# Delta u stored by half units in groups of 32 rows, and spread by two matmuls on different rows of the array

## The chip, the cores and the metric

The program runs on one core of a Trainium2 chip. The metric is the device time of one execution in microseconds, the median of several runs; less is better. The engines are named as in the profile: PE is TensorE (its matmuls; PEld are its weight loads), DVE is VectorE, ACT is ScalarE, POOL is GpSimd, SP is SyncE, which here only issues transfers. SPq and ACTq are the issuing of transfers on SP and ACT.

## The reference, cut to what matters

The program computes four layers on x of shape (4, 96, 64, 64). Layer 0 is a selective scan in four directions, layer 1 a deformable convolution, layers 2 and 3 work on the image as tokens. The change is in layer 0. Its inner part, for each image b, direction k, channel d (192 of them) and state n (16 of them), along l = 0 to 4095:

```python
delta = softplus(dts + delta_bias)
dA = exp(delta[..., None] * A)                       # A: channel x state
h = dA * h + (delta * u)[..., None] * B[:, :, None, :]
y = einsum('bkdn,bkn->bkd', h, C)
```

The product delta * u, a vector over channels, is needed for each of the 16 states of a channel. That repetition is what the text calls spreading.

## The kernel before

**Units.** The scan is cut into 1536 units: 4 images, 4 directions, 4 steps of T = 1024 positions, 3 groups g of 64 channels, and 8 units per group. A unit has 8 channels times 16 states on the 128 partitions, and 1024 positions. Partition p stands for state p // 8 and channel p % 8 of the unit. The 8 units of a group are a block; they are numbered s = i + 4q, with i from 0 to 3 and q from 0 to 1, and are taken in the order i, then q.

**Where delta u comes from.** In `steps` (line 750 on) the softplus and the product with u are made in chunks of CH = 512 positions. The product is written as a sum of three bf16 parts (lines 798 to 808) into the tile `du` of shape [128 channels, 3, 512], or of two halves of 64 channels for two directions. Line 812 stores it in the scratch tensor `du_d[b]`, whose shape is [4 directions, 3 parts, 192 channels, 4096], one or two transfers for each chunk step. The step size itself, delta, is stored in `de_d` (line 794).

**What a unit does.**

- `fetch` (line 911, on ACT's queue) loads the decay tile `da`: 8 rows of `de_d`, each of them to 16 partitions, 512 KB in all. It is done five units ahead.
- `fetch_block` (line 926, on SP's queue) loads delta u for the next block: two tiles of 96 rows (3 parts x 32 channels) by 1024 positions in bf16, one for q = 0 and one for q = 1, 192 KB each. It is issued at the third unit of a block.
- `fetch_step` (line 918, SP) loads B and C for a step, once in 24 units.
- `decay` (line 932, ACT) takes the exponential of `da` with the scale `al`, a column of A for each unit.
- `inflow` (line 938, PE) spreads delta u: two matmuls of 96 rows by 128 columns, one for each half of 512 positions, into the two PSUM banks of a tile `db`. The stationary operand `rep` is a matrix of zeros and ones that picks the 8 channels of the unit from the 32 of the tile, and adds the three parts. The same rows of the array serve both halves. There are two such tiles, four of the eight banks.
- `enter` (line 952, DVE) multiplies `db` by B in place, and `recur` (line 960, DVE) runs the recurrence along the positions.
- `weigh` (line 969, POOL) multiplies by C.
- `total` (line 988, PE) adds the 16 states of a channel for two units at once: eight matmuls with 32 columns, into four column groups, with the matrix `fold`, which also puts each channel at its place among 32. `settle` and `store` (lines 999 and 1006) bring the sums to `y_d`.

**What sets the order.** All instructions are written out in program order, engine by engine. Beside the scan two streams of other work (layer 0's own first and last parts, and layers 1 to 3 of the images that are ready) are cut into steps. A planner, the class `Clock`, keeps a planned end for each engine from costs in the source, and lets a step of a stream in between two units if the engines have room. The spreading of a unit costs PE 0.8 us in this plan (line 935), and a unit has a pace of 4.5 us. So the costs change the order of the instructions, nothing else. After the last unit the streams go on alone; that part is called the tail.

**Completion of transfers.** The transfers of SP and ACT count their completions on eight semaphores in turn (read from the built program). A transfer waits until the one before it on its semaphore has landed.

Of the kernel before, what the change touches and what calls it, by code (L numbers as in the profile page):

```python
# [20 lines left out]
L = H * W  # L21
DI, NS, R, KG = 192, 16, 6, 4
D2 = DI - 128
T = 1024
# [20 lines left out]
def prepare(x, **w):  # L45
# [51 lines left out]
    dtp[64 : 64 + R + 1, 2:] = dtw[2:].transpose(2, 0, 1)  # L97
    a["dtw"] = dtp

    al = w["L0_conv_A_logs"].reshape(KG, DI // D8, D8, NS)  # L100
    a["al"] = c(al.transpose(3, 2, 0, 1).reshape(128, KG * DI // D8))

    ds = w["L0_conv_Ds"].reshape(KG, NG, 64).transpose(2, 1, 0)
    a["ds"] = c(np.concatenate([ds, ds]))
# [22 lines left out]
    for n in (2, 3):  # L127
# [14 lines left out]
    a["cen_c"] = wide(cen[128:], 256)  # L142

    p = np.arange(128)
    rep = (p[:, None, None] % 32 == 8 * np.arange(4)[None, :, None] + p[None, None] % 8).astype(f)
    a["rep"] = c(rep)
    a["fold"] = c(
        (p[:, None, None] % 8 + 8 * np.arange(4)[None, :, None] == np.arange(32)[None, None]).astype(f)
    )
    yy, xx = np.divmod(np.arange(L).reshape(32, 128).T, W)  # L150
    ki, kj = np.divmod(np.arange(9), 3)
# [368 lines left out]
class Unit:  # L520


    def __init__(self, b, k, step, g, i, q):
        self.b, self.k, self.step, self.g, self.i = b, k, step, g, i
        self.s = i + 4 * q
        self.back = k >= 2
        self.j = NT - 1 - step if self.back else step
        self.n = 8 * g + self.s
        self.key = f"{b}_{k}_{self.j}_{g}_{self.s}"
        self.first_of_block = i == 0 and q == 0  # L530
        self.first_of_step = self.first_of_block and g == 0
        self.ts = slice(self.j * T, (self.j + 1) * T)
        self.bc = self.du = None
# [5 lines left out]
class Layer0:  # L539
# [7 lines left out]
    def __init__(self, ctx, net, x1):  # L547
        self.net, self.x1 = net, x1
        tc, nc, ins = net.tc, net.nc, net.ins
        wp = ctx.enter_context(tc.tile_pool(name="l0w", bufs=1))  # L550
        for name in ("fold", "al", "ds"):
            setattr(self, name, net.load(name, wp))

        nc.scalar.activation(self.al, self.al, AF.Exp)
        nc.vector.tensor_scalar_mul(self.al, self.al, -1.0)

        dsum = wp.tile([128, NG], F32, name="dsum")
        nc.vector.reduce_sum(dsum, self.ds, axis=mybir.AxisListType.X)
        self.skip = wp.tile([128, NG, 128], F32, name="skip")
        for g in range(NG):  # L560
            nc.vector.tensor_scalar_mul(self.skip[:, g, :], net.ident, dsum[:, g : g + 1])

        self.wc_d = net.dram.tile([C, 9, 256], F32, name="wc_d")
        self.rep = wp.tile([128, 4, 128], BF16, name="rep16")
        self.minus = wp.tile([128, 128], BF16, name="minus")
        nc.vector.tensor_scalar_mul(self.minus, net.ident, -1.0)
        with tc.tile_pool(name="l0prep", bufs=1) as tp:
            nc.vector.tensor_copy(self.rep, net.load("rep", tp))
            w_in = net.load("w_in", tp)
            cw = tp.tile([C, 9, 256], F32, name="cwr")  # L570
            nc.sync.dma_start(cw, ins["cw"].partition_broadcast(C))
            nc.vector.tensor_mul(cw, cw, w_in[:, :256].unsqueeze(1).to_broadcast([C, 9, 256]))
            nc.sync.dma_start(self.wc_d, cw)
        dram = net.dram
        self.u_d = [dram.tile([DI, L], F32, name=f"u{b}") for b in range(B)]
        self.z_d = [dram.tile([DI, L], F32, name=f"z{b}") for b in range(B)]
        self.de_d = [dram.tile([KG, DI, L], F32, name=f"de{b}") for b in range(B)]
        self.du_d = [dram.tile([KG, 3, DI, L], BF16, name=f"du{b}") for b in range(B)]
        self.bc_d = [dram.tile([KG, 2 * NS, L], F32, name=f"bcd{b}") for b in range(B)]
        self.y_d = [dram.tile([KG, DI, L], F32, name=f"y{b}") for b in range(B)]  # L580
        self.sp = ctx.enter_context(tc.tile_pool(name="l0s", bufs=2))
        self.banks = ctx.enter_context(ExitStack())
        self.ps = self.banks.enter_context(tc.tile_pool(name="l0q", bufs=1, space=PSUM))


        self.ready, self.summed = set(), set()

        self.scanned = (0.0, 0.0)

        self.settled = 0.0  # L590
# [160 lines left out]
    def steps(self, b, ks, j, us, dtw, sm, xdbl):  # L751
# [56 lines left out]
        nc.scalar.copy(du[:, 2, :], pr)  # L808
        yield cost(pe=0.4, act=0.6)
        for p0, p1, k, c0 in parts:  # L810
            dst = self.du_d[b][k][:, c0 : c0 + p1 - p0, cs]
            nc.sync.dma_start(dst.rearrange("s c t -> c s t"), du[p0:p1])
        self.ready.update((b, k, both, j) for k in ks)
        yield wait(frees="du")

# [66 lines left out]
    def fetch(self, u, before):  # L882


        sp, nc = self.sp, self.net.nc
        b, k, j, g, ts = u.b, u.k, u.j, u.g, u.ts
        c0 = 64 * g
        halves = [slice(j * T + h * CH, j * T + (h + 1) * CH) for h in range(2)]
        if not u.first_of_step:
            u.bc = before.bc  # L890
        elif u.bc is None:
            self.fetch_step(u)
        if u.first_of_step and u.step == 0:
            u.state = sp.tile([128, DI // D8], F32, name=f"st{u.key}", tag="st")
        else:
            u.state = before.state
        if not u.first_of_block:
            u.du, u.sums = before.du, before.sums
        else:
            u.sums = {"add": None}  # L900
            if u.du is None:
                self.fetch_block(u)
        if u.i == 1 and u.s == 1 and (k == 0 or u.back):
            add = u.sums["add"] = sp.tile([128, CH], F32, name=f"ad{u.key}", tag="ad", bufs=1)
            src = self.y_d[b][k - 2] if u.back else self.u_d[b]
            for h in range(2):
                nc.scalar.dma_start(add[64 * h : 64 * h + 64], src[c0 : c0 + 64, halves[h]])
        self.net.clock.add(ACT, 0.6, self.scanned[1])
        u.da = sp.tile([128, T], F32, name=f"da{u.key}", tag="da", bufs=6)
        src = self.de_d[b][k][c0 + D8 * u.s : c0 + D8 * u.s + D8, ts]  # L910
        nc.scalar.dma_start(u.da, src.unsqueeze(0).to_broadcast([NS, D8, T]))

    def fetch_step(self, u):
# [5 lines left out]

    def fetch_block(self, u):  # L920

        u.du = []
        for q in range(2):
            t = self.sp.tile([96, T], BF16, name=f"du{u.key}_{q}", tag=f"du{q}")
            c0 = 64 * u.g + 32 * q
            self.net.nc.sync.dma_start(t, self.du_d[u.b][u.k][:, c0 : c0 + 32, u.ts])
            u.du.append(t)

    def decay(self, u):
        u.decayed = self.net.clock.add(ACT, 1.15, 0.0)  # L930
# [1 line left out]
        self.net.nc.scalar.activation(u.da, u.da, AF.Exp, scale=self.al[:, a : a + 1])  # L932

    def inflow(self, u):
        u.spread = self.net.clock.add(PE, 0.8, self.scanned[1])
        db = self.ps.tile([128, 2, CH], F32, name=f"db{u.key}", tag="db", bufs=2)
        for h in range(2):
            self.net.nc.tensor.matmul(  # L938
                db[:, h, :],
                lhsT=self.rep[:96, u.s % 4, :],  # L940
                rhs=u.du[u.s // 4][:, h * CH : (h + 1) * CH],
                start=True,
                stop=True,
            )
        u.db = db.rearrange("p h t -> p (h t)")
# [843 lines left out]
```

## Time and profile before

| | |
|---|---|
| timed runs | 9014.61 us median of 3 (9012.24 to 9038.34) |
| profiled execution, span from first to last instruction | 8965.3 us (no other time of that execution is listed) |
| granted TensorE clock, mean | 0.807 |
| PE busy | 6639.1 us (74%) |
| DVE busy | 6689.3 us (75%) |
| ACT busy | 5244.1 us (58%) |
| POOL busy | 5561.5 us (62%) |
| spreading matmuls (line 938), 3072 | 1101.2 us busy |
| transfers | 1608.49 MB, 179 GB/s in the mean |

The timed runs stand about 49 us above the profiled span, which covers first to last instruction alone. A share of busy time is an average over the whole span; the scan runs from about 350 us to 7634 us, and the tail after it has other limits. In the lists of groups, a row gives line, engine, operation, output and inputs, shape and count, then busy time and the mean of one in nanoseconds, then the idle time of the engine just before such instructions and what ended it. A wait is given as "who <- whom: total, times, longest".

### The profile page before, as it was taken

To read this page: it belongs to the slowest core of one execution; us is meant where nothing else is said; L and a number is where in the kernel's file an instruction comes from. 1 tells how busy PE (TensorE), PEld (TensorE's weight loads), DVE (VectorE), ACT (ScalarE), POOL (GpSimd) and SP (SyncE) were. 2 spreads that over 40 slices of the span, in tenths; PEclk is the share of its full clock that TensorE was granted. 3 is DMA by queue.
4 is the path that set the end of the run, shared out by engine and by line. 5 is a ranking of instruction groups with operands and counts; after the bars stand their busy time and mean duration, and the time that the engine had idled before them with its cause. 6 is when DMAs were issued, how large, how long until landed. Compare 5 with 4: busy or idle time off the path is not lost.

```text
span 8965.3 us, 97776 instructions
## 1 busy us (share of the span) xinstructions
PE 6639.1 (74%) x31960; PEld 2926.8 (33%) x31960; DVE 6689.3 (75%) x4995; ACT 5244.1 (58%) x10214; POOL 5561.5 (62%) x4307
## 2 busy tenths in 40 slices
PE   6675967687767678777667888776888777766687
PEld 2111311122222233312223554122455322454373
DVE  0498889987889987788898887898887889223414
ACT  4564656555567767755566665545666665267623
POOL 0365657666668888766688887667888876245200
PEclk8776977798778889877778888787898887867798
DMA  1476777767778888877788888667888876434120
GB/s 51 133 205 173 193 191 220 198 183 181 189 202 231 235 224 228 204 199 194 200 230 219 233 218 213 160 177 193 215 229 222 216 188 156 104 108 131 57 62 12
DMA packets 776001, 1608.49 MB, mean 179 GB/s; under 512 B 247810, under 2 KB 339358, under 8 KB 773383
## 3 DMA queue, kind: packets, MB, share of 16 engines
q10 hardware_dynamic: 244224, 843.17, 36.4%
q1 hardware_dynamic: 457542, 532.51, 22.0%
q0 software_dynamic: 73728, 226.57, 9.6%
q8 instruction: 257, 4.21, 0.2%
q14 instruction: 250, 2.04, 0.1%
HBM read 1345.62 MB, written 256.29 MB: 179 GB/s over the span
## 4 chain that ended last, share of the span: by engine, by line
PE 35%; DVE 27%; DMA 15%; ACT 10%; issue 7%; POOL 2%; SPq 2%; ACTq 1%; another core or an unknown queue 0%; DVEq 0%; POOLq 0%
DVE hh L960 13%; DVE db L952 7%; DMA du<-du 5%; PE pc L691 4%; PE py L988 4%; ACT g L1312 4%; PE ps L1331 3%; PE db L938 3%; PE f L1425 3%; DMA da<-de 2%; PE pd L1347 2%; POOL hh L969 1%; DMA bc<-bcd 1%; ACT da L932 1%; PE h L1466 1%
## 5 line engine op out<-in xcount | busy, mean ns | idle before, releaser
L969 POOL TENSOR_TENSOR hh<-hh,bc 128x1024 f32<-128x1024 f32 x1536 | 3658.6, 2384 | 351.9 <-DVE hh L960 244.2
L960 DVE TENSOR_TENSOR_SCAN hh<-da,st,db 128x1024 f32<-128x1024 f32 x1152 | 2701.1, 2345 | 229.9 <-PE py L988 86.1
L952 DVE TENSOR_TENSOR db<-db,bc 128x1024 f32<-128x1024 f32 x1536 | 1863.4, 1213 | 523.2 <-PE db L938 517.9
L932 ACT ACTIVATE da<-da,w_al 128x1024 f32<-128x1024 f32 x1536 | 1741.5, 1146 | 641.0 <-DMA da<-de 287.2
L938 PE MATMUL db<-du,rep 96*128 96x512 bf16 x3072 | 1101.2, 447 | 824.6 <-DVE hh L960 764.5
L1301 POOL DMA_INDIRECT g<-table,idx x1152 | 1151.2, 999 | 546.3 <-issue 195.7
L1312 ACT ACTIVATE g<-g,wt 128x96 f32<-128x96 f32 x4608 | 1282.6, 365 | 146.8 <-DMA du<-du 37.3
L988 PE MATMUL py<-hh,w_fold 128*32 128x512 f32 x6144 | 1055.2, 760 | 24.2 <-POOL hh L969 10.7
L960 DVE TENSOR_TENSOR_SCAN hh<-da,db 128x1024 f32<-128x1024 f32 x384 | 877.3, 2285 | 71.9 <-PE py L988 22.1
L1331 PE MATMUL ps<-w_ident,g 128*96 128x128 f32 x3744 | 682.8, 322 | 300.6 <-ACT g L1312 142.7
L938 PEld LDWEIGHTS <-rep 96*128 96x128 bf16 x3072 | 284.3, 107 | 1772.3 <-issue 1139.0
L780 POOL TENSOR_TENSOR lw<-lw,w 128x512 f32<-128x512 f32 x192 | 244.3, 1273 | 820.9 <-DVE w L778 808.7
L1331 PEld LDWEIGHTS ps<-w_ident,g 128*96 128x96 f32 x3744 | 483.2, 142 | 655.0 <-ACT g L1312 255.2
L967 POOL COPY st<-hh 128x1 f32<-128x1 f32 x1152 | 233.3, 202 | 696.0 <-DVE hh L960 637.4
L691 PE MATMUL pc<-pad,wc 96*128 96x512 f32 x1152 | 548.4, 616 | 53.4 <-DMA wc<-wc_d 46.8
L1339 ACT COPY st<-ps 96x384 f32<-96x384 f32 x384 | 180.2, 472 | 395.5 <-PE ps L1331 301.6
L801 PE MATMUL pr<-ex,w_ident 128*128 128x512 f32 x384 | 281.5, 823 | 173.0 <-DVE ex L791 89.8
L778 DVE SCALAR_TENSOR_TENSOR w<-w,ex 128x512 f32<-128x512 f32 x192 | 159.4, 830 | 285.7 <-ACT w L775 285.6
L1318 DVE TENSOR_TENSOR g<-g 128x576 f32<-128x576 f32 x96 | 72.9, 759 | 390.0 <-ACT g L1312 360.5
L691 PEld LDWEIGHTS pc<-pad,wc 96*128 96x128 f32 x1152 | 217.1, 195 | 336.4 <-issue 305.3
L988 PEld LDWEIGHTS py<-hh,w_fold 128*32 128x32 f32 x6144 | 153.9, 122 | 511.0 <-issue 384.4
L769 PE MATMUL pd<-xd,w_dtw 103*64 103x512 f32 (+1 forms) x512 | 267.1, 800 | 66.5 <-DVE rl L782 27.5
(249 smaller groups left out, 8899.5 us busy)
## 6 DMA issues: line engine op xcount, KB each, us to landing
da<-de ACTq DMA_DIRECT2D x1536, 512.0 KB
du<-du SPq DMA_DIRECT2D x512, 192.0 KB
bc<-bcd SPq DMA_DIRECT2D x128, 512.0 KB
du<-du SPq DMA_DIRECT2D x128, 384.0 KB
y<-yb SPq DMA_DIRECT2D x384, 128.0 KB
de<-rl SPq DMA_DIRECT2D x128, 256.0 KB
m<-in_dft SPq DMA_DIRECT2D x128, 256.0 KB
ad<-y ACTq DMA_DIRECT2D x192, 128.0 KB
```

Of the source, the lines that this page charges most:

```text
L691: nc.tensor.matmul(pp, lhsT=wc[:, q, g * 128 : (g + 1) * 128], rhs=pad[:, r0 + dy : r0 + dy + NR, dx : dx + W], start=(q == 0), stop=(q == 8),
L801: nc.tensor.matmul(pr, lhsT=net.ident, rhs=ex, start=True, stop=False)
L932: self.net.nc.scalar.activation(u.da, u.da, AF.Exp, scale=self.al[:, a : a + 1])
L938: self.net.nc.tensor.matmul(db[:, h, :], lhsT=self.rep[:96, u.s % 4, :], rhs=u.du[u.s // 4][:, h * CH : (h + 1) * CH], start=True, stop=True,)
L952: self.net.nc.vector.tensor_mul(u.db, u.db, u.bc[:, 0, :])
L960: nc.vector.tensor_tensor_scan(u.along(u.hh), u.along(u.da), u.along(u.db), first, ALU.mult, ALU.add)
L969: self.net.nc.gpsimd.tensor_mul(u.hh, u.hh, u.bc[:, 1, :])
L988: nc.tensor.matmul(py[p0 : p0 + 32], lhsT=self.fold[:, u.i, :], rhs=hc[:, h * CH : (h + 1) * CH], start=u.sums["add"] is None and u.i == 0 ...
L1301: nc.gpsimd.indirect_dma_start(out=g[:, k, :], out_offset=None, in_=self.tables[b % 2], in_offset=bass.IndirectOffsetOnAxis(ap=idx[:, n : ...
L1312: nc.scalar.activation(pixel, pixel, AF.Identity, scale=wt[:, n, c : c + 1])
L1331: nc.tensor.matmul(pt[:, k, :], lhsT=g[:, k, c * C : (c + 1) * C], rhs=net.ident, is_transpose=True, start=(c == 0), stop=(c == corners - 1),)
L1425: nc.tensor.matmul(pt[64 * part : 64 * part + 64, c, :], lhsT=d[:, :, c0 + c], rhs=matrix[:, 64 * part : 64 * part + 64], start=True, stop ...
```

## The change

The scratch tensor for delta u is laid out anew: for each direction, chunk of 512 positions and group of 32 channels it holds 96 rows of 512 bf16 numbers, which lie together. Row r = 32 s + c is part s of channel c. A half unit is then loaded as 24 partitions with four rows each: partition p holds the rows 4p to 4p + 3, and the row i of these belongs to the channels c with c % 4 = i. So unit i of a group of 32 channels takes every fourth channel, i, i + 4, and so on, instead of eight neighbours.

- **Store** (line 812 before): one transfer for every 32 channels, in place of one for all the channels of a direction.
- **Load** (line 926): one tile with four pieces of 24 partitions, at partitions 0, 32, 64 and 96, for q = 0 and 1 and the halves h = 0 and 1; four transfers of 96 KB in place of two of 192 KB.
- **Spreading** (line 938): the two matmuls of a unit have 24 rows each, at the partitions 64 q and 64 q + 32. They write the two banks of `db` as before. `rep` is now one matrix for all units.
- **Decay load** (line 911): the 8 rows of `de_d` are every fourth one. The columns of `al` and the matrix `fold` follow the new order of channels.
- **Plan**: the spreading costs PE 0.5 us in place of 0.8.

```diff
@@ -97,8 +97,8 @@
     dtp[64 : 64 + R + 1, 2:] = dtw[2:].transpose(2, 0, 1)
     a["dtw"] = dtp
 
-    al = w["L0_conv_A_logs"].reshape(KG, DI // D8, D8, NS)
-    a["al"] = c(al.transpose(3, 2, 0, 1).reshape(128, KG * DI // D8))
+    al = w["L0_conv_A_logs"].reshape(KG, DI // 32, D8, 4, NS)
+    a["al"] = c(al.transpose(4, 2, 0, 1, 3).reshape(128, KG * DI // D8))
 
     ds = w["L0_conv_Ds"].reshape(KG, NG, 64).transpose(2, 1, 0)
     a["ds"] = c(np.concatenate([ds, ds]))
@@ -142,10 +142,9 @@
     a["cen_c"] = wide(cen[128:], 256)
 
     p = np.arange(128)
-    rep = (p[:, None, None] % 32 == 8 * np.arange(4)[None, :, None] + p[None, None] % 8).astype(f)
-    a["rep"] = c(rep)
+    a["rep"] = c((p[:, None] % 8 == p[None] % 8).astype(f))
     a["fold"] = c(
-        (p[:, None, None] % 8 + 8 * np.arange(4)[None, :, None] == np.arange(32)[None, None]).astype(f)
+        (4 * (p[:, None, None] % 8) + np.arange(4)[None, :, None] == np.arange(32)[None, None]).astype(f)
     )
     yy, xx = np.divmod(np.arange(L).reshape(32, 128).T, W)
     ki, kj = np.divmod(np.arange(9), 3)
@@ -522,6 +521,7 @@
 
     def __init__(self, b, k, step, g, i, q):
         self.b, self.k, self.step, self.g, self.i = b, k, step, g, i
+        self.q = q
         self.s = i + 4 * q
         self.back = k >= 2
         self.j = NT - 1 - step if self.back else step
@@ -561,7 +561,7 @@
             nc.vector.tensor_scalar_mul(self.skip[:, g, :], net.ident, dsum[:, g : g + 1])
 
         self.wc_d = net.dram.tile([C, 9, 256], F32, name="wc_d")
-        self.rep = wp.tile([128, 4, 128], BF16, name="rep16")
+        self.rep = wp.tile([128, 128], BF16, name="rep16")
         self.minus = wp.tile([128, 128], BF16, name="minus")
         nc.vector.tensor_scalar_mul(self.minus, net.ident, -1.0)
         with tc.tile_pool(name="l0prep", bufs=1) as tp:
@@ -575,7 +575,9 @@
         self.u_d = [dram.tile([DI, L], F32, name=f"u{b}") for b in range(B)]
         self.z_d = [dram.tile([DI, L], F32, name=f"z{b}") for b in range(B)]
         self.de_d = [dram.tile([KG, DI, L], F32, name=f"de{b}") for b in range(B)]
-        self.du_d = [dram.tile([KG, 3, DI, L], BF16, name=f"du{b}") for b in range(B)]
+        
+
+        self.du_d = [dram.tile([KG, NCH, DI // 32, 3 * 32, CH], BF16, name=f"du{b}") for b in range(B)]
         self.bc_d = [dram.tile([KG, 2 * NS, L], F32, name=f"bcd{b}") for b in range(B)]
         self.y_d = [dram.tile([KG, DI, L], F32, name=f"y{b}") for b in range(B)]
         self.sp = ctx.enter_context(tc.tile_pool(name="l0s", bufs=2))
@@ -808,8 +810,9 @@
         nc.scalar.copy(du[:, 2, :], pr)
         yield cost(pe=0.4, act=0.6)
         for p0, p1, k, c0 in parts:
-            dst = self.du_d[b][k][:, c0 : c0 + p1 - p0, cs]
-            nc.sync.dma_start(dst.rearrange("s c t -> c s t"), du[p0:p1])
+            for p in range(p0, p1, 32):
+                dst = self.du_d[b][k, j, (c0 + p - p0) // 32].rearrange("(s c) t -> c s t", s=3)
+                nc.sync.dma_start(dst, du[p : p + 32])
         self.ready.update((b, k, both, j) for k in ks)
         yield wait(frees="du")
 
@@ -907,7 +910,7 @@
                 nc.scalar.dma_start(add[64 * h : 64 * h + 64], src[c0 : c0 + 64, halves[h]])
         self.net.clock.add(ACT, 0.6, self.scanned[1])
         u.da = sp.tile([128, T], F32, name=f"da{u.key}", tag="da", bufs=6)
-        src = self.de_d[b][k][c0 + D8 * u.s : c0 + D8 * u.s + D8, ts]
+        src = self.de_d[b][k][c0 + 32 * u.q + u.i : c0 + 32 * u.q + 32 : 4, ts]
         nc.scalar.dma_start(u.da, src.unsqueeze(0).to_broadcast([NS, D8, T]))
 
     def fetch_step(self, u):
@@ -919,12 +922,12 @@
 
     def fetch_block(self, u):
 
-        u.du = []
+        u.du = self.sp.tile([128, 4, CH], BF16, name=f"du{u.key}", tag="du")
         for q in range(2):
-            t = self.sp.tile([96, T], BF16, name=f"du{u.key}_{q}", tag=f"du{q}")
-            c0 = 64 * u.g + 32 * q
-            self.net.nc.sync.dma_start(t, self.du_d[u.b][u.k][:, c0 : c0 + 32, u.ts])
-            u.du.append(t)
+            for h in range(2):
+                p0 = 64 * q + 32 * h
+                src = self.du_d[u.b][u.k, 2 * u.j + h, 2 * u.g + q]
+                self.net.nc.sync.dma_start(u.du[p0 : p0 + 24], src.rearrange("(p i) t -> p i t", i=4))
 
     def decay(self, u):
         u.decayed = self.net.clock.add(ACT, 1.15, 0.0)
@@ -932,13 +935,13 @@
         self.net.nc.scalar.activation(u.da, u.da, AF.Exp, scale=self.al[:, a : a + 1])
 
     def inflow(self, u):
-        u.spread = self.net.clock.add(PE, 0.8, self.scanned[1])
+        u.spread = self.net.clock.add(PE, 0.5, self.scanned[1])
         db = self.ps.tile([128, 2, CH], F32, name=f"db{u.key}", tag="db", bufs=2)
         for h in range(2):
             self.net.nc.tensor.matmul(
                 db[:, h, :],
-                lhsT=self.rep[:96, u.s % 4, :],
-                rhs=u.du[u.s // 4][:, h * CH : (h + 1) * CH],
+                lhsT=self.rep[64 * u.q + 32 * h : 64 * u.q + 32 * h + 24],
+                rhs=u.du[64 * u.q + 32 * h : 64 * u.q + 32 * h + 24, u.i, :],
                 start=True,
                 stop=True,
             )
```

## Prediction

> **What bounds the kernel now.** I read the page first, then the busy time of the stage that the change touches, then the list of waits, then the chain piece by piece.
>
> ```profile
> PE 6639.1 (74%) x31960; PEld 2926.8 (33%) x31960; DVE 6689.3 (75%) x4995; ACT 5244.1 (58%) x10214; POOL 5561.5 (62%) x4307
> ...
> PE 35%; DVE 27%; DMA 15%; ACT 10%; issue 7%; POOL 2%; SPq 2%; ACTq 1%; another core or an unknown queue 0%; DVEq 0%; POOLq 0%
> ...
> L952 DVE TENSOR_TENSOR db<-db,bc 128x1024 f32<-128x1024 f32 x1536 | 1863.4, 1213 | 523.2 <-PE db L938 517.9
> ...
> L938 PE MATMUL db<-du,rep 96*128 96x512 bf16 x3072 | 1101.2, 447 | 824.6 <-DVE hh L960 764.5
> ```
>
> No engine is full over the span; the chain is mostly PE and DVE handing over to each other. Its second line (by line) gives DMA du<-du 5% and PE db L938 3%, the two things that the change touches. The scan runs from 350 to 7634 us:
>
> ```profile
> 350.00:7634.00 7284.00, 5455.65 (x24581) 2175.05 (x24582) 6247.82 (x4239) 4443.47 (x8179) 5228.19 (x3975) 0.81 0.78 203
> ```
>
> The columns after the length are PE, PEld, DVE, ACT, POOL busy, the clock and the DMA share. DVE (third) is busy 86% there, so it sets the pace and only its 7284 - 6248 = 1036 us of idle time can be won in this stage. The waits, each with its total, count and longest:
>
> ```profile
> DVE db L952 <- PE db L938: 517.9, 226, 20.6
> ...
> ACT da L932 <- DMA da<-de: 287.2, 136, 9.8
> ...
> PE db L938 <- DMA du<-du: 40.5, 8, 22.4
> ```
>
> Half of DVE's idle time is the wait for the spread (226 times, 2.3 us each). The pair itself takes 0.61 us, so most of such a wait is PE being late for another reason. One is seen in the chain:
>
> ```profile
> 5169.87 0.55 ACTq L911
> 5170.42 0.05 issue
> 5170.47 0.17 ACT g L1312
> 5170.63 21.44 DMA du<-du
> 5192.07 0.02 issue
> 5192.09 0.02 ACTq L911
> ```
>
> Nothing on ACT reads du here. ACT issues the next decay load (L911), and in the program as built the loads and stores of SP and ACT take eight completion semaphores in turn: each waits for the landing of the one eight before it. A slow du load so stops ACT, and with it whatever PE waits for from ACT. From the issue and completion times in the trace: a du load (192 KB) lands after 12.6 us in the mean (5% above 22.1), a decay load of 512 KB after 7.6 us. ACT's issues stood 425 us in all on such semaphores, 184 us of it (54 times) on a du load.
>
> **What the Trainium skill says.** "DMA: Bandwidth & Descriptors", section "Why a DMA increments its semaphore by 16 and not by 1": a transfer runs on the largest number of engines up to 16 that divides the slowest dimension of both sides. A du load reads 3 x 32 x 1024 into 96 rows, so 3 engines. The trace agrees: 4 increments (3 and the sequencer's rest) at the median against 16 for the others. After the change it is 24 rows on both sides, so 12. "TensorEngine Tiling (Array Packing)", "Key Properties": changing the tiling mode drains TensorE. The trace agrees: from the second spread matmul to a full-array one (L1331, L691) is 215 ns, start to start, to the column-tiled fold (L988) 307 ns; leaving the fold for the spread costs 525 against 429. A switch is 92 to 97 ns. "TensorE: Matmul & The Clock Gate", Part 3: matmuls on different row groups start about 4 ns apart. The trace has no pair on different rows; its column-tiled folds start 6 to 7 ns apart.
>
> **The change part by part.**
>
> *The pair on PE (L938).* Now the second matmul of a pair starts 219 to 226 ns after the first. On different rows and banks I take 7 ns, the fold's figure: 212 x 1536 units = -326 us of PE. The bound on the other side: K=64 matmuls that follow each other on the same rows (L1059) start 533 ns apart where full-array ones need 429, so a weight load that cannot be hidden shows as 104 ns. With a gap of 110 ns it is -167 us. If the two do not overlap at all, 0. Below -326 is excluded, since one of the two still streams.
>
> *Mode switches.* The pair is now a 32-row mode. In the built programs the matmul stream changes mode 2508 times before and 3858 after: +1350 x 92 ns = +124 us of PE. Where PE was waiting anyhow it costs nothing; where the granted clock is half it costs double. PE in sum: -202 us (-43 with the unhidden load, +124 without overlap). PE is 35% of the chain, so **-70 us** (-15 to +43).
>
> *The du loads.* Two of 192 KB on 3 engines become four of 96 KB on 12: per engine 128 KB becomes 32 KB, and the mean landing of 12.6 us, for two that share 3 engines, becomes about 5 us (a quarter of it, and the 2 us that the smallest transfers here take). Three waits shrink. ACT's 184 us on du semaphores: less two thirds, -120. ACT's wait for decay data: a decay load lands in 8.7 us when a du load is in flight (883 of 1536) and 6.2 us when not; the 16-engine load waits for the three busy engines. Most of that difference goes, half of the 287 us: -140. PE's own waits for du, 41 us and 34 more at its weight load: -50. In sum -310 us of engine waits. They lie beside DVE's work except where they reach it; I let the share of the PE chain, 0.35 to 0.4, through: **-120 us** (0, if DVE is held by the next late thing each time, to -250).
>
> *More transfers on eight semaphores.* Loads +384, stores +512 (a step's one or two become four of 32 rows): 2550 on SP become 3446, with 1824 on ACT unchanged. The time until a semaphore comes round, 11.8 us at the median for a decay load before 4750 us, falls by a fifth to 9.8 us. Queued behind are SP's stores of y and loads of bc and, on ACT, the exponentials. The other 241 us of ACT's semaphore waits grow by about a third, +85, of which 0.4 counts: **+35 us** (0 to +150).
>
> *SP's issues.* 896 x 0.63 us (1610 us for 2550 now) = 560 us more, 18% to 24% of the span. Hidden by SP's idle time; without that cover each burst delays the next issue by 1 to 2 us: 0 to +20.
>
> *Decay loads with rows 64 KiB apart instead of 16.* Same 4 KB rows, same 16 engines. The Trainium skill, "DMA: Bandwidth & Descriptors", "Latency and other measured facts", sees copies slow down above a pitch of 512 KiB, not shown here: 0, up to +30.
>
> *Order and planner (0.8 becomes 0.5).* DVE instructions after the last scan fall from 687 to 656: side work comes earlier by little. The sign of a reshuffled order is open: 0, -40 to +40. The multiply now comes before side work on DVE more often (713 such instructions stand between multiply and scan, 640 before): a wait there is the price if the spread is late.
>
> Sum: -70 - 120 + 35 = **-155 us**. The profiled span 8965.3 gives 8810; the page lists no time of that execution beside its span. The median of the timed runs, 9014.61, lies 49.3 us above the span, taken as unchanged: **8860 us**. What is late next is the scan on DVE itself, and PE with the offset and sampling matmuls (L1331, L1425).
>
> **Rivals.**
>
> *Only one half works.* Either the pair overlaps but the switches take it back, or the loads land sooner but DVE waits for something else: about half of the sum, -45 to -85 us, 8930 to 8970. For it: the next waits are close behind (fold's hh buffers 108 us). Against it: two separate mechanisms would have to fail in turn.
>
> *Slower: the semaphores come round too soon.* Bursts of four stores and four loads take half of the eight at once, and ACT waits at its next decay load. It decides if a transfer lands later than the eighth issue after it, 9.8 us: a decay load's 95th percentile is already 11.4 us in the first stage. 192 load bursts and 192 store bursts with 1 us on ACT each are 384 us, times 0.4 is +150; with -70 on PE and the du gain gone, 9014.6 + 80 = 9095, and 9050 if half of the bursts are hit. Against it: the same bytes in smaller pieces land sooner, and the longest holders, the du loads, are the ones cut.
>
> *No overlap on rows.* The matmuls stay 219 ns apart, and the 124 us of switches are added: +43, with -85 from the loads 8970. The profile has no row pair to exclude it.
>
> *Nothing to see.* DVE refills each gap: within 27 us of 9014.6.
>
> **How the numbers follow.** Both halves 0.50 (8860, own range 8780 to 8930); one half or no overlap on rows 0.20 (8930 to 8980); nothing 0.11; slower 0.19 (9050 to 9100). Faster by over 0.3% (27 us, about what a measurement of this kernel can tell from no change) is 0.70, within it 0.11, slower 0.19. The range leaves out about one in ten above and one below: 8760 to 9045.
>
> **What would show it.** Right: the pair's PE row drops from 1101 us busy to about 600 to 750; du loads land in about 5 us; du<-du falls from 5% of the chain to under 2%; ACT's wait for da from 287 to about 150 us; DVE's for db from 518 to 350 to 400; the scan stage ends 130 to 170 us sooner and the tail stays at about 1330 us. Wrong: the matmuls of a pair over 200 ns apart; ACT's semaphore waits above 425 us; or DVE's idle time in the scan unchanged at about 1000 us though both rows improved.

## The result, and the profile after

| | before | after |
|---|---|---|
| timed runs, median | 9013.42 us (4 runs, 8998.19 to 9038.34) | 8902.61 us (4 runs, 8878.90 to 8935.01) |
| profiled span | 8965.3 us | 8907.3 us |
| granted TensorE clock, mean | 0.807 | 0.772 |
| PE busy | 6639.1 us | 6652.8 us |

The medians differ by 111 us, where 154 was forecast. The ratio on record is 0.9894, with a 95% interval of 0.9865 to 0.9923, or 96 us of 9013; it is not the quotient of the two medians, which is 0.9877. All ratios below are of the recorded kind. The two spans differ by 58 us only. In the runs after, an execution takes 1.8 to 1.9 us longer than its span (8909.16 beside 8907.3). So the profiled execution of before took some 8967 us by the same allowance and was a quick one among its runs. The comparisons further on ran on several chips, where the kernel before took between 8940 and 9013 us, so all that is compared across them is compared as a ratio to the runs of before on the same chip. Where an expectation below is in microseconds and reckons from 9013, the ratio is what to hold against it.

From the page of the kernel after, its busy line and four groups (columns as in the rows shown before: busy time, mean ns, idle time before it and what ended that):

```profile
PE 6652.8 (75%) x31960; PEld 2892.8 (32%) x31960; DVE 6650.0 (75%) x4995; ACT 5235.3 (59%) x10214; POOL 5574.2 (63%) x4307
...
L955 DVE TENSOR_TENSOR db<-db,bc 128x1024 f32<-128x1024 f32 x1536 | 1863.3, 1213 | 574.3 <-PE db L941 553.6
L935 ACT ACTIVATE da<-da,w_al 128x1024 f32<-128x1024 f32 x1536 | 1739.3, 1146 | 492.1 <-DMA da<-de 134.6
...
L941 PE MATMUL db<-du,rep 24*128 24x512 bf16 x3072 | 707.8, 459 | 869.5 <-DVE hh L963 803.8
...
L991 PE MATMUL py<-hh,w_fold 128*32 128x512 f32 x6144 | 1119.7, 798 | 20.5 <-POOL hh L972 13.6
```

The spreading fell from 1101 to 708 us busy, 393 us less. But PE as a whole did not fall. Its other work rose from 6639.1 - 1101.2 = 5537.9 to 6652.8 - 707.8 = 5945.0 us, 407 us more, with the same 31960 matmuls. The fold (L991) is one row of it, 798 ns for one after; before it was 760 ns:

```profile
L988 PE MATMUL py<-hh,w_fold 128*32 128x512 f32 x6144 | 1055.2, 760 | 24.2 <-POOL hh L969 10.7
```

ACT's wait for decay data halved, from 287 to 135 us. DVE's wait for the spread was to fall and rose, from 518 to 554 us.

In one stretch of the timeline the two matmuls of a unit begin together and take 0.39 us, with the fold straight after; before, such a pair took 0.61 us:

```profile
5263.69 0.39 PE L941 MATMUL db<-du,rep 24*128 24x512 bf16 x2
...
5264.01 1.06 PE L991 MATMUL py<-hh,w_fold 128*32 128x512 f32 x8
```

Next the scan and the tail. The columns are the window, its length, the busy time and count of PE, PEld, DVE, ACT and POOL, the granted clock, the DMA share and GB/s. This is the kernel after, its windows split at the end of the scan:

```profile
350.00:7652.00 7302.00, 5522.94 (x25493) 2188.44 (x25493) 6235.57 (x4271) 4462.94 (x8229) 5240.55 (x3977) 0.77 0.80 204
7652.00:8907.30 1255.30, 912.64 (x6018) 619.81 (x6018) 375.75 (x655) 616.70 (x1792) 318.79 (x312) 0.77 0.28 78
```

And the kernel before, split at the end of its own scan:

```profile
350.00:7637.00 7287.00, 5458.34 (x24594) 2175.35 (x24594) 6250.69 (x4241) 4443.47 (x8179) 5229.99 (x3975) 0.81 0.78 203
7637.00:8965.30 1328.30, 969.55 (x6916) 668.38 (x6916) 399.61 (x686) 644.73 (x1842) 316.65 (x313) 0.79 0.28 80
```

The scan did not get shorter: it ends 15 us later. DVE is idle 7302 - 6236 = 1066 us in it, where it was 7287 - 6251 = 1036. The tail is 73 us shorter, and some 900 matmuls (25493 against 24594) have moved from the tail into the scan. So three things had to be explained: PE's other work that grew, a scan that gained nothing from better loads, and a gain that shows in the tail.

### The profile page after: what moved, and what is told of

It reads as the page before. It is cut to its first block, busy times and chain, and to the rows that moved or that the text cites. A ratio compares the mean times of both kernels' runs of the same rounds, so it can differ in the third digit from the quotient of the medians.

```text
span 8907.3 us, 98649 instructions
## 1 busy us (share of the span) xinstructions
PE 6652.8 (75%) x31960; PEld 2892.8 (32%) x31960; DVE 6650.0 (75%) x4995; ACT 5235.3 (59%) x10214; POOL 5574.2 (63%) x4307
## 4 chain that ended last, share of the span: by engine, by line
PE 23%; DVE 14%; ACT 9%; DMA 7%; issue 5%; POOL 2%; SPq 1%; ACTq 1%; another core or an unknown queue 0%; DVEq 0%; POOLq 0%
DVE hh L963 7%; ACT g L1315 4%; DVE db L955 3%; PE f L1428 3%; PE ps L1334 3%; PE py L991 2%; DMA da<-de 2%; PE pd L1350 2%; DMA m<-in_dft 1%; ACT da L935 1%; PE db L941 1%; POOL hh L972 1%; PE zp L1494 1%; PE h L1469 1%; PE pc L693 1%
## 5 line engine op out<-in xcount | busy, mean ns | idle before, releaser
L935 ACT ACTIVATE da<-da,w_al 128x1024 f32<-128x1024 f32 x1536 | 1739.3, 1146 | 492.1 <-DMA da<-de 134.6
L941 PE MATMUL db<-du,rep 24*128 24x512 bf16 x3072 | 707.8, 459 | 869.5 <-DVE hh L963 803.8
L991 PE MATMUL py<-hh,w_fold 128*32 128x512 f32 x6144 | 1119.7, 798 | 20.5 <-POOL hh L972 13.6
L941 PEld LDWEIGHTS <-rep 24*128 24x128 bf16 x3072 | 159.5, 93 | 1979.8 <-issue 1222.5
L803 PE MATMUL pr<-ex,w_ident 128*128 128x512 f32 x384 | 320.8, 930 | 178.3 <-DVE ex L793 96.0
L771 PE MATMUL pd<-xd,w_dtw 103*64 103x512 f32 (+1 forms) x512 | 296.7, 879 | 72.6 <-DVE rl L784 31.1
L1350 PE MATMUL pd<-st,wdc 96*128 96x256 f32 x1152 | 327.1, 436 | 9.6 <-DVE rl L784 4.9
```

Source lines behind the costliest of these rows:

```text
L803: nc.tensor.matmul(pr, lhsT=net.ident, rhs=ex, start=True, stop=False)
L941: self.net.nc.tensor.matmul(db[:, h, :], lhsT=self.rep[64 * u.q + 32 * h : 64 * u.q + 32 * h + 24], rhs=u.du[64 * u.q + 32 * h : 64 * u.q ...
L991: nc.tensor.matmul(py[p0 : p0 + 32], lhsT=self.fold[:, u.i, :], rhs=hc[:, h * CH : (h + 1) * CH], start=u.sums["add"] is None and u.i == 0 ...
L1350: nc.tensor.matmul(po, lhsT=wdc[:, k, :], rhs=st[:, k, :], start=(k == 0), stop=(k == 8))
```

## The experiments

The change has four separable parts: loads spread over more DMA engines, more and smaller transfers, the pair on different rows, and the plan value 0.5. My theory was that the loads and the pair both gain. The rivals were that one of the two does nothing, that the transfers take the gain back, or that the plan does more than assumed. The edits are shown cut to the lines that matter for the argument; `...` stands for lines left out.

### The loads alone

The kernel before, with nothing changed but the order of the dimensions of `du_d`, so that one run of 96 rows is read; the store and the matrix `rep` follow that order. Two loads a block and 0.8 in the plan stay.

```diff
-du_d: [KG, 3, DI, L]
+du_d: [KG, DI, 3, L]
...
-dma_start(t, self.du_d[u.b][u.k][:, c0 : c0 + 32, u.ts])
+src = self.du_d[u.b][u.k][c0 : c0 + 32, :, u.ts]
+dma_start(t, src.rearrange("c s t -> (c s) t"))
...
-rep = (p[:, None, None] % 32 == ...)
+rep = (p[:, None, None] // 3 == ...)
...
```

> The kernel before, with delta u stored as [direction, channel, part, position], so that a load of 32 channels has 96 rows in its slowest dimension on both sides (16 engines in place of 3). Two loads of 192 KB and as many stores as before, the spreading on the full array and the plan (0.8) as before. The loads theory (the gain of 111 us comes from du loads that leave three engines): 8900 to 8940 us, du loads landing in 5 to 7 us, ACT's wait for da near 135 us. The pair theory (it comes from the overlap of the two spreading matmuls) and the plan theory (it comes from the cost 0.5): within 27 us of before, 8990 to 9040.

Measured: 8761.58 us, ratio 0.9757 (0.9730 to 0.9784). That is more than the whole change brings, and more than expected. A du load now makes 16 completion increments in place of 4 and lands after 6.5 us in the mean (12.6 before). Decay loads land after 7.0 us (7.6 before), B and C after 10.2 (15.5). ACT stands on completion semaphores for 202 us in place of 425, of which 22 in place of 184 are on du loads. In the list of waits of this kernel (who, for whom, total, times, longest) DVE's wait for the spread is down from 518 us, though PE does the same matmuls:

```profile
DVE db L952 <- PE db L938: 386.4, 193, 17.8
...
ACT da L932 <- DMA da<-de: 208.0, 101, 8.0
```

And its windows, scan and tail:

```profile
350.00:7405.00 7055.00, 5413.64 (x24594) 2165.26 (x24594) 6245.81 (x4240) 4440.99 (x8181) 5234.99 (x3975) 0.81 0.81 210
7405.00:8736.40 1331.40, 973.48 (x6918) 672.40 (x6916) 400.06 (x687) 644.47 (x1842) 317.25 (x313) 0.79 0.28 79
```

The scan ends 232 us earlier and the tail is untouched. So the late loads had been in the path of the scan all along.

### The change without the better loads

The kernel after, with an empty 33rd row in each part of the scratch tensor, so that parts cannot be read as one run and a load falls back to 3 engines.

```diff
-du_d: [KG, NCH, DI // 32, 3 * 32, CH]
+du_d: [KG, NCH, DI // 32, 3, 33, CH]
...
-dma_start(u.du[p0 : p0 + 24], src.rearrange("(p i) t -> p i t", i=4))
+src = src[:, :32].rearrange("s (c i) t -> s c i t", i=4)
+dma_start(u.du[p0 : p0 + 24], src)
```

> The kernel after, with one spare row of 512 positions behind each part of 32 channels in the scratch tensor, so that a load's source has 3 as its slowest dimension and runs on 3 engines again; pieces, sizes, PE work and plan as in after. Loads theory: the gain is gone, 9000 to 9080 us, since the mode switches and the 896 additional transfers stay. Pair theory and plan theory: about as after, 8885 to 8925.

Measured: 9069.62 us, ratio 1.0097 (1.0065 to 1.0130). With 4 increments a load lands after 9.3 us (6.0 in the kernel after, with 13). The decay loads land after 7.6 us (6.9 in the kernel after), B and C after 13.6 (9.4), with pieces of the same size. Without the better loads the other parts together make the kernel slower. So the pair, the plan and the transfers are a net loss.

### The plan value, in both kernels

`add(PE, 0.5, ...)` in the kernel before, in place of 0.8:

> The kernel before with one number changed: the planned cost of spreading 0.5 in place of 0.8. Plan theory: 8900 to 8950 us, with more of image 2's work ahead of the tail. Loads theory and pair theory: within 27 us of before, or slower, since PE then has more work in front of a spread that takes as long as it did.

Measured: 9027.98 us (20 runs), ratio 1.0040 (1.0027 to 1.0053). And 0.8 in the kernel after, in place of 0.5:

> The kernel after with the planned cost of spreading back at 0.8. The run of before with 0.5 was 0.4% slower than before, so if the plan costs the same here, 35 us less than after: 8860 to 8885 us. If the plan's cost only arises with a spread that takes long (it is short here), no difference to after: 8885 to 8920.

Measured: 8785.95 us, ratio 0.9811 (0.9792 to 0.9831), where the kernel after has 0.9894: twice the 0.4% that was expected. Scan and tail of this last kernel:

```profile
350.00:7478.00 7128.00, 5398.15 (x24594) 2108.02 (x24594) 6249.12 (x4240) 4442.49 (x8179) 5234.16 (x3975) 0.77 0.82 208
7478.00:8787.90 1309.90, 989.97 (x6918) 684.27 (x6916) 399.83 (x687) 644.21 (x1842) 317.40 (x313) 0.78 0.29 81
```

With 0.8 the scan ends 159 us earlier than before, in the forecast's 130 to 170, and the tail takes 1310 us (1328 before). The same shift shows in the kernel before with 0.5:

```profile
350.00:7768.00 7418.00, 5553.70 (x25492) 2257.51 (x25492) 6229.07 (x4271) 4464.74 (x8229) 5237.44 (x3977) 0.81 0.77 200
7768.00:9022.70 1254.70, 909.76 (x6025) 616.91 (x6018) 375.92 (x655) 616.77 (x1793) 320.32 (x312) 0.78 0.28 78
```

Its scan is 131 us longer and its tail 74 us shorter. The lower value lets side work (900 matmuls, 30 instructions of DVE) in earlier. There it costs more than it saves later. It also takes a share of ACT's wait for decay data, though no load has changed (287.2 us before):

```profile
ACT da L932 <- DMA da<-de: 217.7, 109, 6.2
```

The moved work is why the scan of the kernel after seemed to gain nothing, and why the gain showed in the tail.

To see whether a still higher value gains, the loads-alone kernel with 1.1 in place of 0.8:

> The run with loads on 16 engines with the planned cost of spreading at 1.1 in place of 0.8. Going from 0.8 to 0.5 cost 0.4% in the kernel before and 0.8% with the new layout. If a plan that holds less PE work ahead of a spread is better throughout, this one gains by 0.2 to 0.6% on the loads alone: 0.970 to 0.974 of before. If 0.8 is near the best value: 0.975 to 0.982.

Measured: 8793.82 us, ratio 0.9830 (0.9810 to 0.9851), where the same kernel with 0.8 has 0.9757. The scan ends at 7302 us, the earliest of all, but the tail takes 1492 us. So 0.8 is better than 1.1 here, and better than 0.5 in the three kernels in which that was tried (before, after, and the full-array kernel below).

### The pair: whole array, rows and columns

To take the pair's overlap away and keep the layout, the loads, the transfers and the plan of the kernel after: 96 rows hold all four pieces, and each matmul uses all of them with a matrix that is zero outside its own 24. So no row mode is used and nothing overlaps.

```diff
...
-p0 = 64 * q + 32 * h
+p0 = 24 * (2 * q + h)
-lhsT=self.rep[64 * u.q + 32 * h : 64 * u.q + 32 * h + 24],
-rhs=u.du[64 * u.q + 32 * h : 64 * u.q + 32 * h + 24, u.i, :],
+lhsT=self.rep[:96, 2 * u.q + h],
+rhs=u.du[:, u.i, :],
```

> The kernel after with the four pieces of a block at partitions 0, 24, 48 and 72, and the spreading done by full-array matmuls of 96 rows whose stationary matrix is zero outside the 24 rows of the half unit. Transfers, layout and plan as in after; no pair on different rows, no change of mode. Pair theory: most of the gain is gone, 8990 to 9015 us. Loads theory: 8870 to 8930 us. Clock: if the 24-row pairs are what lowered the granted clock (0.772 in after's profile, 0.807 in before's), it is back near 0.80.

Measured: 8886.36 us, ratio 0.9882 (0.9854 to 0.9910), beside 0.9894 for the kernel after. The same with 0.8 in the plan:

> The kernel after with full-array spreading (as in the run with pieces at partitions 0, 24, 48, 72) and the plan at 0.8. Beside the run of after with 0.8 it is the second measurement of the pair: if the pair is worth nothing, both lie within 20 us of each other, 8840 to 8885. If the pair is worth what its matmuls save (393 us busy on PE, a third of it on the path), this one is over 100 us slower.

Measured: 8773.17 us, ratio 0.9810 (0.9793 to 0.9826), beside 0.9811 for the kernel after with 0.8, on the same chip. The pair on different rows gains nothing that can be measured in either plan. These last two kernels differ in the pair alone (and in the partitions that its pieces lie on), so the 400 us can be followed. Busy PE and the spreading matmuls of the full array, then of rows, from their pages:

```profile
PE 6607.9 (75%) x31960; PEld 2916.1 (33%) x31960; DVE 6688.1 (76%) x4995; ACT 5238.7 (60%) x10214; POOL 5562.8 (63%) x4307
...
L942 PE MATMUL db<-du,rep 96*128 96x512 bf16 x3072 | 1100.9, 447 | 840.1 <-DVE hh L964 774.0
```

```profile
PE 6605.7 (75%) x31960; PEld 2876.8 (33%) x31960; DVE 6687.6 (76%) x4995; ACT 5242.4 (60%) x10214; POOL 5566.4 (63%) x4307
...
L941 PE MATMUL db<-du,rep 24*128 24x512 bf16 x3072 | 705.0, 458 | 878.7 <-DVE hh L963 836.3
```

Other work on PE: 6607.9 - 1100.9 = 5507.0 against 6605.7 - 705.0 = 5900.7 us. The rows save 396 us and lose 394. The loss can be seen on matmuls that have no part in the change. The part sums of delta u (`pr`), from the view of one tile, with the shortest, median and longest duration in ns, first with the full array, then with rows:

```profile
L804 PE MATMUL pr<-ex,w_ident x384: 590/697/1223, 284.5 to 4679.2; 128*128 128x512 f32 x192
```

```profile
L803 PE MATMUL pr<-ex,w_ident x384: 590/1059/1222, 283.8 to 4694.3; 128*128 128x512 f32 x192
```

The shortest and the longest are the same; the median goes from 697 to 1059 ns. So more of them ran slow, at up to twice the shortest time. The mean granted clock of the whole execution says the same, the full array's first:

```profile
core 0: 8760.8 us, clock 0.812
```

```profile
core 0: 8787.9 us, clock 0.774
```

The fall is in the scan alone (0.82 against 0.77); the tail, which has no spreading, has 0.78 in both. The rows are shown above; the full array's are:

```profile
350.00:7461.00 7111.00, 5414.63 (x24594) 2153.25 (x24594) 6250.31 (x4241) 4438.72 (x8179) 5231.34 (x3976) 0.82 0.82 208
7461.00:8760.80 1299.80, 980.19 (x6916) 679.33 (x6916) 398.80 (x686) 644.12 (x1842) 316.63 (x313) 0.78 0.29 81
```

The traces also hold the clock's own records: it is at full or at half, in intervals of 3.41 us. In all 13 traces no interval of the scan in which PE was busy for under 40% was followed by one at full clock (0 of 4091). After intervals without any spreading the clock was full about as often in both kernels (227 of 495 with the full array, 270 of 572 with rows). After intervals with PE busy for 90% or more, at least a tenth of the interval with spreading, it was full in 94% of cases with the full array and in 82% with rows (706 of 752, 562 of 683). So the clock is lost in the intervals that follow spreading on rows, at the same busy share of PE.

An estimate of the 394 us from these numbers: 5507 us at 0.774 in place of 0.812 are 5777, or 270 us more. The 1350 more mode switches (counted in the kernel after) at 92 to 99 ns (the start to start of a spread matmul and its neighbour with a change of mode, less that without one) are 124 to 134 us more. Together 394 to 404. It adds up, but the clock's part is shared out by a mean over the span, so the split stays an estimate.

Is it the overlap that lowers the clock? The kernel after with both matmuls of a unit on the same 48 rows, again with a masked matrix; then they cannot overlap.

```diff
...
-p0 = 64 * q + 32 * h
+p0 = 64 * q + 24 * h
-lhsT=self.rep[64 * u.q + 32 * h : 64 * u.q + 32 * h + 24],
-rhs=u.du[64 * u.q + 32 * h : 64 * u.q + 32 * h + 24, u.i, :],
+lhsT=self.rep[64 * u.q : 64 * u.q + 48, h],
+rhs=u.du[64 * u.q : 64 * u.q + 48, u.i, :],
```

> The kernel after with the two pieces of a half unit at 64 q and 64 q + 24, so that both matmuls of a unit read the same 48 rows (the matrix is zero on the other 24) and cannot overlap; changes of mode as in after. If the clock falls because a part of the rows is used, it stays near 0.77 here; if it falls because the array is at work for a shorter time (two matmuls at once), it is back near 0.80. Time: the two stand some 320 ns apart in place of 4, 490 us more on PE, a third on the path: 9000 to 9080 us, or about 60 us less if the clock is back.

Measured: 8987.23 us, ratio 1.0050 (1.0032 to 1.0068). From its page and its view of cores:

```profile
PE 6957.2 (78%) x31960; PEld 2895.1 (32%) x31960; DVE 6655.8 (74%) x4995; ACT 5239.5 (58%) x10214; POOL 5571.2 (62%) x4307
...
L942 PE MATMUL db<-du,rep 48*128 48x512 bf16 x3072 | 1114.6, 455 | 760.6 <-DVE hh L964 718.6
```

```profile
core 0: 8968.6 us, clock 0.781
```

The matmuls of a pair are 226 ns apart (320 had been expected), PE is busier than in any other kernel, and the clock is still low (0.776 to 0.782 over its runs, 0.774 to 0.781 for the overlapping pair on the same chip). So the overlap is not needed for a low clock. Nor is it the zeros in the matrix, which the full-array kernel has too, at 0.807. This run also splits the pair's effect. Leaving the full array for a row mode costs 1.0050 / 0.9882, 1.7%. The overlap then wins 1.0050 back to 0.9894, 1.6%.

Is it the number of mode switches? The loads-alone kernel with each spreading matmul cut into two column halves: 96 rows, so no row mode, but a column mode that fits neither the offset matmuls nor the fold. The stream changes mode 3620 times, against 2508 in the loads-alone kernel and 3858 in the kernel after.

```diff
+for m in range(2):
+    ms = slice(64 * m, 64 * m + 64)
-        db[:, h, :], lhsT=self.rep[:96, u.s % 4, :],
+        db[ms, h, :], lhsT=self.rep[:96, u.s % 4, ms],
```

> The run with loads on 16 engines (clock 0.810, 0.9757 of before), its spreading split by columns: four matmuls of 96 rows by 64 columns for a unit, so the array changes its mode about as often as in after (3620 times in the program; after 3858, loads alone 2508) while all 96 rows stay in use. If the changes of mode lower the granted clock, it is near 0.775; if rows in use do, it stays near 0.81. Time, where the clock stays: 1112 changes at 92 ns are 102 us of PE and the unhidden weight loads 80 us more, 0.3 of it on the path: 0.6% above the loads alone, 0.982 of before; with the lower clock 0.990.

Measured: 8738.55 us, ratio 0.9775 (0.9755 to 0.9796). From its views of cores and of the tile `pr`:

```profile
core 0: 8737.8 us, clock 0.816
```

```profile
L801 PE MATMUL pr<-ex,w_ident x384: 590/697/1222, 284.6 to 4657.4; 128*128 128x512 f32 x192
```

The clock stays up (0.814 to 0.819 over its runs) and the median of `pr` stays at 697 ns. The switches of this run, which are changes of the column mode, do not lower the clock, and the 1112 more switches cost at most little: 0.9775 against 0.9757, with intervals that overlap.

### The number of transfers

The loads-alone kernel with as many transfers as the kernel after: loads in two halves of 512 positions, stores of 32 channels, 896 transfers more.

```diff
...
-dma_start(self.du_d[b][k][c0 : c0 + p1 - p0, :, cs], du[p0:p1])
+for p in range(p0, p1, 32):
+    dma_start(self.du_d[b][k][c0 + p - p0 : c0 + p - p0 + 32, :, cs], du[p : p + 32])
...
+for h in range(2):
+    hs = slice(u.j * T + h * CH, u.j * T + (h + 1) * CH)
-    src = self.du_d[u.b][u.k][c0 : c0 + 32, :, u.ts]
-    dma_start(t, ...)
+    src = self.du_d[u.b][u.k][c0 : c0 + 32, :, hs]
+    dma_start(t[:, h * CH : (h + 1) * CH], ...)
```

> The run with loads on 16 engines (8762 us, 0.9757 of before) with its transfers split as in after: a load of 192 KB into two of 96 KB, each still on 16 engines, a store into one for every 32 channels; PE and plan (0.8) as before, channels in their old order. If the 896 additional transfers on the eight semaphores are what after loses against the loads alone, 8830 to 8870 us. If they cost nothing, and the new order of channels or 24 rows in place of 96 do, 8750 to 8780.

Measured: 8782.81 us, ratio 0.9812 (0.9792 to 0.9831), which is 0.55% above the loads alone (8844 of 9013 us, within the 8830 to 8870 of the first case), though the loads land sooner (5.6 us). ACT stands on completion semaphores for some 340 us, where it stood for 202. Loads and stores were split in one run, so which of the two costs the time is open. The full-array kernel of the new layout with 0.8 has 0.9810, so the new order of channels, the spacing of the decay rows and the 24-row pieces together add nothing to it.

In the other direction, the loads-alone kernel with one load of 384 KB for a block, in place of two of 192 KB:

> The run with loads on 16 engines with one load of 384 KB for a block in place of two of 192 KB: 192 transfers fewer on the eight semaphores. 896 more cost 0.55% of before, so in proportion it gains 0.1%: 0.9735 to 0.976 of before, at the edge of what five rounds tell. If the larger piece holds its semaphore too long, it is slower by as much: 0.976 to 0.979.

Measured: 8726.26 us, ratio 0.9757 (0.9734 to 0.9781), the same as with two. It repeats the gain of the loads on another chip. 192 transfers fewer gain nothing that can be measured; in proportion to the 896 it would be 0.1%, which these runs can hardly tell. This and the loads-alone kernel are the best versions found, 2.4% below before and 1.4% below the kernel after.

### The parts together

| step | from ratio | to ratio | in us, of 9013 |
|---|---|---|---|
| loads on 16 engines | 1 | 0.9757 | -219 |
| 896 more transfers | 0.9757 | 0.9812 | +50 |
| new layout, order, 24-row pieces | 0.9812 | 0.9810 | about 0 |
| pair on different rows | 0.9810 | 0.9811 | about 0 |
| plan 0.8 to 0.5 | 0.9811 | 0.9894 | +75 |

The steps follow each other from kernel to kernel, so they add up by construction, to 0.9894 and some 95 us. Each interval is about 0.2 to 0.3% to either side, so the size of the transfers' step is loose, some 20 to 80 us. The third and the fourth lie within one comparison. The last is seen twice more: 0.9810 to 0.9882 with the full array, and +0.4% in the kernel before.

## Why the prediction was right, and where its sum was not

It said faster, 8860 us within 8760 to 9045, and 8902.61 was measured. The direction came from the loads, as it said. But the sum came out near by errors that cancel: against the table of parts the loads were 99 us too small, the pair 70 and the plan 75 us too good, and the transfers 15. That the result fell into 8780 to 8930, which was kept for both halves at work, was luck, since one half brought nothing.

- **The loads, -120 us: the mechanism right, the size too small.** A mean landing of about 5 us was forecast, 6.0 measured; ACT's semaphore waits fell from 425 to 196 us, and those on du loads from 184 to 36. What the skill says in "DMA: Bandwidth & Descriptors", section "Why a DMA increments its semaphore by 16 and not by 1" (the slowest dimension sets how many engines a transfer runs on), held in the runs: 4, 13 and 16 increments for 3, 12 and 16 engines. ACT's wait for decay data was to fall to about 150 us and is at 134.6, but only in part through the loads: the loads alone leave it at 208.0, and the plan alone, with the old loads, at 217.7. The forecast took the gap between 8.7 us (a du load in flight) and 6.2 us (none) as the harm that the three engines do. With du loads on 16 engines the same split still shows 8.0 and 6.3 us, so most of the gap is something else. The term that was mis-sized is the share of the waits let through to the end, 0.35 to 0.4 of 310 us. With the loads alone the three waits of the sum fell by some 274 us (162 on du semaphores, 79 for decay data, 33 on PE) and the kernel by 219 us, 0.8 of them.
- **The pair, -70 us: this step failed.** PE in sum was to fall by 202 us; with the plan at 0.8 it falls by 2 (6605.7 against 6607.9). Its inputs were right: 3 to 4 ns between the two starts ("TensorE: Matmul & The Clock Gate", Part 3, has about 4 ns), a switch of 92 to 99 ns ("TensorEngine Tiling (Array Packing)", "Key Properties", has the drain without a price), a row of 600 to 750 us busy (707.8). What the sum lacked is a clock that depends on how the array is used. Apart from the switches it took the other 5538 us of PE as fixed, and they became 5945. A lower granted clock was nowhere among its bounds or rivals. The share of 0.35 for PE time was not at fault: from the kernel with 48 rows to the kernel after, 1536 pairs lose 226 - 4 = 222 ns, 341 us of PE (304 us in its busy time), and the ratio falls by 1.56%, some 140 us, a share of 0.41 (0.46).
- **More transfers, +35 us:** +50 in the runs, inside its bounds. That it comes through ACT's semaphore waits is not shown: they rose from 202 to some 340 us when the transfers were added to the loads-alone kernel, but are some 230 us in the full-array kernel with 0.8, which has as many transfers and the same ratio.
- **SP's issues and the decay rows, 0 each:** nothing speaks against it. SP's issues can't be told apart from the +50 of the transfers; the decay rows are part of the third step of the table, about 0.
- **The plan, 0 with -40 to +40: wrong in the kernel after**, +75 us, and at +36 inside the bound in the kernel before. I had seen 31 DVE instructions move and called them little. The 900 matmuls that moved with them were not counted. Why they cost more in the scan than they save in the tail was not taken further.
- **The signs in the scan failed.** The scan was to end 130 to 170 us sooner, with the tail the same, DVE's wait for the spread at 350 to 400 us and its idle time below 1000. All of this is what the kernel with 0.8 shows, or nearly so (159 us sooner, a tail of 1310 us, 406.8 us of wait, 7128 - 6249 = 879 us idle). The prediction's own test, DVE's idle time unchanged although the PE row and ACT's wait got better, was met by the kernel after. It pointed to the plan, not to the loads.
- **du<-du under 2% of the chain** can't be judged in the kernel after, whose chain can be followed through some 60% of the span only. With 0.8 in the plan, where it is whole, du<-du has 2% (5% before).
- **The 49 us around the span** were spread between executions. They did not touch the sum, which was taken as a difference.

Of the rivals, "only one half works" is what happened, with the loads whole and at nearly twice their price; its 8930 to 8970 was too high for that reason. "Semaphores come round too soon" was right that more transfers cost something, at a third of its price. The kernel with 3 engines shows what it would have taken to end on that side: 1.0097 of before, with no gain from the loads.

What stays open: which property of a row mode lowers the granted clock. It is not overlap, not zeros in the matrix, and not the number of switches as far as those of a column mode can show it. 24 and 48 rows were tried, both at 128 columns. That PE's work might count by the rows in use fits the intervals above, but no run tests it.

## What to carry to other kernels

Before anything else, count the DMA engines that each recurring load runs on: one reordered dimension of a scratch tensor was worth more than the whole change here (0.9757 against 0.9894), and other loads landed sooner with it. Price a change of matmul shape on the granted clock and on all other work of PE, not on its own row alone; a row that gets 400 us shorter can leave the engine as busy as before. And try a planner's constant apart from the change that it comes with.

## What the runs showed of the hardware that was not expected

**Partial rows lowered the granted clock.** With 24 or 48 rows for the spreading the mean clock lies at 0.762 to 0.782 over all runs of these kernels; with the full array, zeros or not, or with half the columns, at 0.798 to 0.819. The fall is in the scan, where the spreading runs (0.82 to 0.77 in the two kernels with 0.8), and not in the tail (0.78 in both). It costs matmuls that have nothing to do with the packed ones: the median of `pr` goes from 697 to 1059 ns.

**Few-engine transfers slow the others.** With du loads on 16 engines in place of 3 the decay loads, which run on 16 in both, landed after 7.0 us in place of 7.6, and B and C after 10.2 in place of 15.5. In the new layout, 3 engines in place of 12 took them from 6.9 to 7.6 and from 9.4 to 13.6 us. That a decay load takes 8.7 us beside a du load on 3 engines and 6.2 us otherwise does not measure this effect: beside one on 16 engines it still takes 8.0 us, otherwise 6.3.
